# Masked attention rewritten in the form of the two unmasked layers

## The chip, the cores and the metric

The kernel runs on one core of one Trainium2 chip, in one launch. The metric is the device time of that launch in microseconds. Five engines work beside each other, each on its own queue in order: TensorE (PE; its weight loads are PEld), VectorE (DVE), ScalarE (ACT), GpSimd (POOL) and SyncE (SP), which issues most of the DMAs. Semaphores order work between the queues.

## The reference

Four blocks, each a gated cross attention followed by a gated feed-forward part, work on x of shape (16, 112, 256) with a context of shape (16, 375, 256). The change touches the second attention alone:

```python
scores = jnp.einsum('bhqd,bhkd->bhqk', q, k) * scale
scores = jnp.clip(scores, -100.0, 100.0)
scores = jnp.where(mask == 0, -jnp.inf, scores)
attn = jax.nn.softmax(scores, axis=-1)
out = jnp.einsum('bhqk,bhkd->bhqd', attn, v)
```

There are 16 heads of 16 columns. The first and third attentions are the same without clip and mask. The fourth has one head. The feed-forward parts of the first two blocks are mixtures of eight experts, of which each row uses two; the third is a feed-forward part of eight dense experts, the fourth a quantised one. All arithmetic is fp32 on the chip, apart from small bf16 helpers.

## The kernel before

One function, `attention`, makes the three many-headed layers. The context lies in SBUF for all 16 batches, transposed (`ctxT`). Layer by layer a loop runs over the batches b. Four batches form a group of queries: normalised, transposed and projected together (`norm_part`, `rows_part`, `both_queries_T`, `both_queries`). Keys and values of a batch are projected a batch or two ahead. The heads are handled in units `cp` of four: a head has 16 rows, two neighbours share 32 rows of TensorE, and the queries are masked so that one of the two counts.

The order on PE, ACT, DVE and POOL is written out by hand (`tc.manual_schedule`); only the SP queue is left to the scheduler. PSUM has two pools: three pairs of banks, `wide`, and two single ones, `bank`. A step that wants a pair waits until the third pair before it has been read out.

The unmasked layers 0 and 2 (`unmasked`) compute the scores twice. `maxima` computes them with the queries on the partitions, 112x375 a head, two heads in a pair, and VectorE reduces a pair to two negated maxima (L455). `max_parts` splits the maxima into three bf16 parts on GpSimd, and `max_rows` turns them (L475). `exponentials(b, i)`, three a batch, computes the scores again with the keys on the partitions, 125x224 a matmul into two pairs (L490), subtracts the maxima by a matmul of ones with the three parts (L502), and ScalarE takes the exponential out of PSUM (L511). `weighted` multiplies them with the values, beside which stand columns of ones, so that the sums come out too. `normalised` divides on VectorE (L545 to L553), `output` projects and adds.

The masked layer 1 (`with_mask`) computes the scores once, queries on the partitions. VectorE clips a pair and applies the mask in one pass out of PSUM (L602), then reduces it (L619). ScalarE exponentiates each head with its maximum as bias and its sum as accumulator output (L622). TensorE turns the weights, six transposes for two heads (L634), ScalarE or VectorE copies them out (L638), and `weighted_masked` multiplies with the values (L651). The inverse sums are spread to the columns on GpSimd (L666) and turned on TensorE (L675). A zero column stands behind the 375 context rows, so that a row with nothing valid stays finite.

The mixtures of layers 0 and 1 are worked off in between. `fill()` advances three generators by one step each: `route` (which expert, and scattering the rows by indirect DMA), `products` (a tile of 128 rows a step: a matmul with the expert's weights and the transpose of the next tile, one `wide` pair, L1170 and L1180) and `combine` (gather and add, L1208). A group's mixture begins when `ready` enters it, and `ensure` forces what is left of a group before the next layer needs it. So mixture work of layer 0 lies in layers 0 and 1, that of layer 1 in layers 1 and 2. The numbers of `fill()` calls decide which.

Steps that the change touches: `maxima`, `max_parts`, `max_rows`, `exponentials`, `weighted`, `output`, `mask_of`, `values_of`, `both_keys`, and the loops `unmasked` and `with_mask`.

Of the kernel before, what the change touches and what calls it, by code (L numbers as in the profile page):

```python
# [13 lines left out]
I32 = mybir.dt.int32  # L14
# [33 lines left out]
def tile_gated_xattn_stack(ctx: ExitStack, tc: tile.TileContext, a: dict, out: bass.AP):  # L48
# [22 lines left out]

    ctxZ = [ctxp.tile([P, 2, T + 1], F32, tag=f"ctx{b}", name=f"ctx{b}") for b in range(B)]
    ctxT = [t[:, :, :T] for t in ctxZ]
# [4 lines left out]
    def load_ctx(b):  # L78
        nc.gpsimd.memset(ctxZ[b][:, :, T:], 0.0)
        nc.sync.dma_start(ctxT[b], a["ctx"][:, :, b * T : (b + 1) * T])  # L80
# [173 lines left out]
    CTS = [(c, t) for c in range(2) for t in range(NT)]  # L254

    def attention(pool, layer, w):
# [6 lines left out]
        rss, uppers, valss = {}, {}, {}  # L263
        masked = layer == 1
        TK = T + 1 if masked else T
# [84 lines left out]
        def keys_of(b, c):  # L350
            if b >= B:
                return
            if c == 0:
                kTs[b] = pool.tile([P, 2, T + 1], F32, tag="kT", name=f"kT_{L}_{b}", bufs=3)
            pk = bank(f"pk_{L}_{b}_{c}")
            project(pk, w["wk"], c, ctxZ[b], TK)
            nc.scalar.activation(kTs[b][:, c, :TK], pk[:, :TK], AF.Identity, bias=w["bk"][:, c : c + 1])

        def both_keys(b):
            if b >= B:  # L360
                return
            kT = kTs[b] = pool.tile([P, 2, T + 1], F32, tag="kT", name=f"kT_{L}_{b}", bufs=3)
            pk = wide(f"pk_{L}_{b}")
            for c in range(2):
                project(pk[:, c, :], w["wk"], c, ctxZ[b], TK)
            if "bk" in w:
                for c in range(2):
                    nc.scalar.activation(kT[:, c, :TK], pk[:, c, :TK], AF.Identity, bias=w["bk"][:, c : c + 1])
            else:
                nc.scalar.copy(kT[:, :, :TK], pk[:, :, :TK])  # L370

# [26 lines left out]
        def values_of(b, ts):  # L398
# [15 lines left out]
            def copies():  # L414
                for i, t in enumerate(ts):
                    (nc.vector.tensor_copy if masked else nc.scalar.copy)(  # L416
# [12 lines left out]
        def scores(b, cp):  # L429
# [4 lines left out]
            for h in range(2):  # L434
                ps = wide(f"ps_{L}_{b}_{cp}_{h}")
                for i in range(2):
# [3 lines left out]
                        ps[:S, i, :TK],  # L440
                        qms[g][rows, c, p, j * S : (j + 1) * S],
                        kTs[b][rows, c, :TK],
# [6 lines left out]
        def maxima(b, cp):  # L449
            if b >= B:  # L450
                return
            if cp == 0:
                nms[b] = small.tile([S, 4, 4], F32, tag="nm", name=f"nm_{L}_{b}")
            for h, ps in enumerate(scores(b, cp)):
                nc.vector.tensor_reduce(nms[b][:, cp, 2 * h : 2 * h + 2], ps[:S, :, :T], AX.X, ALU.max, negate=True)  # L455

        def max_parts(b):
            if b >= B:
                return
            mp, nm = mparts[b % 2], nms[b]  # L460
            rest = nm
# [7 lines left out]
        def max_rows(b):  # L469
# [9 lines left out]
            nc.scalar.copy(mr, pt[:, : 4 * S].rearrange("p (c s) -> p c s", s=S))  # L479

        def exponentials(b, i):
# [28 lines left out]
            for h in range(2):  # L510
                nc.scalar.activation(  # L511
                    e[:, 2 * h : 2 * h + 2].rearrange("t r q p s -> t r (q p s)"), pairs[h][:TC, :, : 4 * S], AF.Exp
                )

        def weighted(b, i):
# [18 lines left out]
            if i == 2:  # L534
                by_pair = po[:, : 4 * S].rearrange("q (c p s) -> q c p s", p=2, s=S)
                valss[b] = pool.tile([P, 2, S], F32, tag="vals", name=f"vals_{L}_{b}")
# [19 lines left out]
        def output(b):  # L556
# [4 lines left out]
            if masked and b + 1 < B:  # L561

                pos[b + 1] = bank(f"po_{L}_{b + 1}")
                py = pos[b + 1][:, 2 * P :]
            else:
                py = bank(f"py_{L}_{b}")
            for c in range(2):
                nc.tensor.matmul(py[:S, :D], oT[:, c, :], w["wo"][:, c, :], start=(c == 0), stop=(c == 1))
            if not masked:
                xb = x[g][:, j, :]  # L570
                nc.vector.scalar_tensor_tensor(xb, py[:S, :D], gate[:S, layer : layer + 1], xb, ALU.mult, ALU.add)  # L571
                return
            return py

        def output_added(b, py):
            if b < 0:
                return
            g, j = divmod(b, G)
            y = pool.tile([S, D], F32, tag="y", name=f"y_{L}_{b}", bufs=1)
            nc.scalar.mul(y, py[:S, :D], gate[:S, layer : layer + 1])  # L580
# [1276 lines left out]
```

## Time and profile before

| | us |
|---|---|
| median of 7 runs (lowest to highest) | 1588.85 (1584.58 to 1593.59) |
| the profiled execution | 1585.48 |
| its span, first to last instruction | 1583.7 |
| TensorE busy | 1468.8 (93%) |
| VectorE busy | 977.6 (62%) |
| ScalarE busy | 776.2 (49%) |
| GpSimd busy | 603.4 (38%) |

The rows of groups read: line, engine, operation, output and inputs by the program's names, shapes (partitions x elements, type), count, then busy time in us, mean ns of one, and the idle time of the engine just before them with what ended it. Matmuls overlap: the busy time of a group is that of their union, and much smaller than count times mean. Every fp32 matmul of the program stands there as two records. The clock is what TensorE was granted, 1.00 is full. The timeline gives start, length, engine, line, operation and count; in brackets the idle time before and what ended it.

The stretches by layer on the profiled execution: layer 0 and the loads ahead of it end at 388.4 us, where the first scores of the masked layer begin; the scores of layer 2 begin at 868.2, the dense experts about 1222.6.

### The profile page before, as it was taken

What the parts mean: (1) busy time and instruction counts of PE and PEld (TensorE: products, weight loads), DVE (VectorE), ACT (ScalarE), POOL (GpSimd) and SP (SyncE); (2) the same over time, 40 slices, a digit from 0 to 9 for tenths busy, and PEclk for the clock granted to TensorE, in tenths of its full rate; (3) what the DMA queues carried; (4) which work ended last, traced back from release to release, by engine and by line L of the source; (5) the groups of instructions that cost most, each with busy time, mean ns of one, the idle gap of its engine ahead of it and who ended that gap; (6) DMA issues with size and microseconds to landing.
All of it is one profiled execution on the core that took longest, in us unless ns stands there. A gap on an engine that the chain in (4) does not pass through costs nothing.

```text
span 1583.7 us, 34920 instructions
## 1 busy us (share of the span) xinstructions
PE 1468.8 (93%) x13404; PEld 1023.3 (65%) x13404; DVE 977.6 (62%) x1857; ACT 776.2 (49%) x1547; POOL 603.4 (38%) x1079
## 2 busy tenths in 40 slices
PE   7999999999899899998987999999999999899997
PEld 4555666666666666766765666666566887667765
DVE  3566754666776775786683465466555434486775
ACT  2443434445666666666664344444445333465522
POOL 1222133344546545536544235342112434243342
PEclk9899999999999999999998999999999999999999
DMA  9780024253353452534513324410003441100000
GB/s 260 249 269 1 2 81 126 79 158 102 96 153 95 124 147 81 146 91 120 150 51 93 105 83 132 132 52 8 8 8 138 163 149 36 27 16 22 14 10 18
DMA packets 127214, 150.32 MB, mean 95 GB/s; under 512 B 13496, under 2 KB 118280, under 8 KB 125000
## 3 DMA queue, kind: packets, MB, share of 16 engines
q1 hardware_dynamic: 120472, 133.40, 28.5%
q0 software_dynamic: 6144, 14.69, 3.1%
q8 instruction: 106, 1.74, 0.5%
q14 instruction: 60, 0.49, 0.1%
q10 hardware_dynamic: 432, 0.01, 0.0%
HBM read 103.75 MB, written 44.30 MB: 93 GB/s over the span
## 4 chain that ended last, share of the span: by engine, by line
PE 51%; DVE 10%; POOL 5%; ACT 4%; issue 2%; DMA 1%; SPq 1%; POOLq 0%; ACTq 0%; DVEq 0%
PE ps L439 5%; PE pm_m L1170 5%; PE pv L406 4%; PE pe L634 4%; PE pk L231 4%; PE py_f L1328 3%; PE ph L1312 3%; PE pgu_h L1659 2%; PE po L651 2%; PE pt L490 2%; PE po L526 2%; DVE sm L602 2%; PE py L1693 2%; PE pq L231 1%; PE pz L1590 1%
## 5 line engine op out<-in xcount | busy, mean ns | idle before, releaser
L455 DVE TENSOR_REDUCE nm<-ps 112x2 f32<-112x750 f32 x256 | 230.1, 933 | 187.2 <-PE ps L439 186.5
L439 PE MATMUL ps<-kT,qm 32*112 32x375 f32 (+1 forms) x1536 | 213.8, 527 | 19.9 <-ACT ex L511 14.8
L511 ACT ACTIVATE ex<-pt 125x896 f32<-125x896 f32 x192 | 165.7, 914 | 70.8 <-PE pt L502 70.7
L622 ACT ACTIVATE sm<-sm,nmax 112x375 f32<-112x375 f32 x256 | 152.4, 600 | 6.6 <-DVE nmax L619 6.6
L602 DVE SCALAR_TENSOR_TENSOR sm<-ps,up 112x752 f32<-112x752 f32 x128 | 114.5, 934 | 65.6 <-PE ps L439 58.3
L634 PE MATMUL pe<-ident,sm 112*125 112x112 f32 x768 | 116.4, 286 | 29.3 <-DVE sm L602 15.1
L634 PEld LDWEIGHTS pe<-ident,sm 112*125 112x125 f32 x768 | 104.1, 196 | 57.6 <-ACT sm L622 41.9
L1170 PE MATMUL pm_m<-w_m,xy_m 128*128 128x256 f32 x416 | 117.4, 405 | 11.5 <-DVE sm L602 3.9
L439 PEld LDWEIGHTS ps<-kT,qm 32*112 32x112 f32 x1536 | 72.6, 173 | 76.7 <-ACT ex L511 33.8
L490 PE MATMUL pt<-qm,kT 32*125 32x224 f32 x1536 | 116.1, 382 | 3.7 <-DVE nm L455 2.0
L1153 POOL TENSOR_TENSOR xy_m<-xy_m,wb_m 128x256 f32<-128x256 f32 x112 | 82.2, 735 | 97.0 <-ACT xy_m L1182 96.2
L1182 ACT COPY xy_m<-pm_m 128x512 f32<-128x512 f32 x112 | 63.3, 566 | 107.2 <-PE pm_m L1180 58.4
L619 DVE TENSOR_REDUCE nmax<-sm 112x2 f32<-112x752 f32 x128 | 113.0, 923 | 0.0
L427 POOL TENSOR_SCALAR oT<-oT,w_L_xattn_bv 128x112 f32<-128x112 f32 x64 | 36.3, 575 | 191.6 <-DVE oT L553 122.4
L1170 PEld LDWEIGHTS pm_m<-w_m,xy_m 128*128 128x128 f32 x416 | 72.6, 192 | 50.4 <-ACT eT L638 15.6
L526 PE MATMUL po<-ex,vpad 125*32 125x112 f32 x3072 | 98.4, 270 | 1.6 <-ACT vpad L416 0.7
L406 PE MATMUL pv<-w_L_xattn_wv,ctx 128*125 128x256 f32 x384 | 97.4, 390 | 1.1 <-DVE x L571 1.0
L490 PEld LDWEIGHTS pt<-qm,kT 32*125 32x125 f32 x1536 | 74.7, 186 | 31.4 <-issue 12.7
L231 PE MATMUL pk<-ctx,w_L_xattn_wk 128*128 128x376 f32 (+1 forms) x256 | 93.1, 498 | 0.9 <-ACT qm L392 0.9
L638 ACT COPY eT<-pe 125x672 f32<-125x672 f32 x96 | 68.9, 718 | 51.0 <-PE pe L634 48.4
L526 PEld LDWEIGHTS po<-ex,vpad 125*32 125x32 f32 x3072 | 74.0, 113 | 28.9 <-issue 21.3
L406 PEld LDWEIGHTS pv<-w_L_xattn_wv,ctx 128*125 128x125 f32 x384 | 67.7, 188 | 23.1 <-issue 8.6
(328 smaller groups left out, 2816.5 us busy)
## 6 DMA issues: line engine op xcount, KB each, us to landing
w_m<-in_L_ffn_expert_w_dram SPq DMA_DIRECT2D x112, 256.0 KB, 3.8
w<-in_L_ffn_w_dram SPq DMA_DIRECT2D x16, 1024.0 KB, 5.8
xg_m<-rows_in SPq DMA_DIRECT2D x112, 128.0 KB, 2.7
wb_m<-in_L_ffn_expert_b_dram SPq DMA_DIRECT2D x112, 128.0 KB, 3.8
rows_out<-xy_m SPq DMA_DIRECT2D x112, 128.0 KB, 1.8
rows_in<-zero SPq DMA_DIRECT2D x2, 4992.0 KB
rows_out<-zero SPq DMA_DIRECT2D x2, 4992.0 KB
ctx<-in_ctx_dram SPq DMA_DIRECT2D x16, 375.0 KB, 9.5
```

The lines of the kernel that those rows point to most:

```text
L231: nc.tensor.matmul(ps[:, :n], w[:, k, c * P : (c + 1) * P], rhs[:, k, :n], start=(k == 0), stop=(k == 1))
L406: nc.tensor.matmul(pv[:TC, i * D : (i + 1) * D], rhs_of(b)[:, k, t * TC : (t + 1) * TC], w["wv"][:, k, :], start=(k == 0), stop=(k == 1),)
L439: nc.tensor.matmul(ps[:S, i, :TK], qms[g][rows, c, p, j * S : (j + 1) * S], kTs[b][rows, c, :TK], start=True, stop=True,)
L455: nc.vector.tensor_reduce(nms[b][:, cp, 2 * h : 2 * h + 2], ps[:S, :, :T], AX.X, ALU.max, negate=True)
L490: nc.tensor.matmul(pairs[r // 2][:TC, r % 2, q * 2 * S : (q + 1) * 2 * S], kTs[b][rows, c, t * TC : (t + 1) * TC], qms[g][rows, c, :, j * ...
L511: nc.scalar.activation(e[:, 2 * h : 2 * h + 2].rearrange("t r q p s -> t r (q p s)"), pairs[h][:TC, :, : 4 * S], AF.Exp)
L526: nc.tensor.matmul(po[32 * r : 32 * r + 32, (2 * c + p) * S : (2 * c + p + 1) * S], vp[:, t, 4 * c + r, p : p + 2, :], e[:, r, q, p, :], s ...
L602: nc.vector.scalar_tensor_tensor(sm[:, 2 * h : 2 * h + 2, :], ps[:S, :, :TK], -100.0, uppers[b][:, None, :].to_broadcast([S, 2, TK]), ALU.max,
L619: nc.vector.tensor_reduce(part, sm[:, 2 * h : 2 * h + 2, :], AX.X, ALU.max, negate=True)
L622: nc.scalar.activation(sm[:, i, :T], sm[:, i, :T], AF.Exp, bias=nmax[:, i : i + 1], accum_out=rss[b][:, head : head + 1])
L634: nc.tensor.transpose(pt[:TC, i, t * S : (t + 1) * S], sm[:, 2 * h + i, t * TC : (t + 1) * TC], ident[:S, :S])
L1170: nc.tensor.matmul(pt[:, 1, :D], xgT[:, k * P : (k + 1) * P], w[:, k * D : (k + 1) * D], start=(k == 0), stop=(k == 1),)
```

## The change

The masked layer takes the form of the two others; one loop, `run`, serves all three. What differs in it for the masked layer:

- The mask of a batch is loaded one batch ahead (`load_mask`), and GpSimd turns it into a bf16 tile `ups` of 0 and -1e30 (one pass in place of two and a memset).
- `maxima`: one fused instruction a head adds that tile to the scores and takes the maximum, 16 a batch in place of eight reductions. The sum goes to a scratch tile `over` of one buffer. In the changed program's order each stands as two instructions, the pass and a read of the accumulator into `nm`, and most passes wait for an earlier instruction of VectorE's own queue.
- `max_parts` first clips the maxima to between -20 and 100 on GpSimd.
- `max_rows` also turns the mask (four bf16 transposes, one third twice, so that any two neighbouring thirds stand side by side) and ScalarE copies it twice.
- `exponentials`: VectorE clips and masks what the two matmuls left in PSUM in one pass (at least -80, at most 0 or -1e30) and writes it to SBUF; ScalarE takes the exponential there in place.
- The value copies of the masked layer go to ScalarE. The zero column of the context is gone.

In the shared loop, layers 1 and 2 start the norm of the next group one batch later (`when`), batch 15 has two more `fill()`s in every layer, and the masked layer one more in every fourth batch. A masked batch has five `fill()`s, each fourth six; before it had six.

```diff
+    LOW = 20.0
...
             for h, ps in enumerate(scores(b, cp)):
-                nc.vector.tensor_reduce(nms[b][:, cp, 2 * h : 2 * h + 2], ps[:S, :, :T], AX.X, ALU.max, negate=True)
+                if not masked:
+                    nc.vector.tensor_reduce(nms[b][:, cp, 2 * h : 2 * h + 2], ps[:S, :, :T], AX.X, ALU.max, negate=True)
+                    continue
+                for i in range(2):
+                    r = 2 * h + i
+                    over = pool.tile([S, T], F32, tag="over", name=f"over_{L}_{b}_{cp}_{r}", bufs=1)
+                    nc.vector.tensor_tensor_reduce(
+                        over, ps[:S, i, :T], ups[b], 1.0, -3.0e38, ALU.add, ALU.max, nms[b][:, cp, r : r + 1]
+                    )
...
+            if masked:
+
+                rest = small.tile([S, 4, 4], F32, tag="left", name=f"cut_{L}_{b}")
+                nc.gpsimd.tensor_scalar(rest, nms[b], -LOW, 100.0, ALU.max, ALU.min)
...
+            up = ups.pop(b)
+            for i in range(4):
+                t = i % NT
+                nc.tensor.transpose(pt[:TC, (4 + i) * S : (5 + i) * S], up[:, t * TC : (t + 1) * TC], identb[:S, :S])
+            nc.scalar.mul(mr, by_unit, -1.0)
+            uT = uTs[b] = pool.tile([TC, 4, 2, S], BF16, tag="uT", name=f"uT_{L}_{b}")
+            for p in range(2):
+                nc.scalar.copy(uT[:, :, p, :], pt[:TC, 4 * S : 8 * S].rearrange("t (i s) -> t i s", s=S))
...
             for h in range(2):
-                nc.scalar.activation(
-                    e[:, 2 * h : 2 * h + 2].rearrange("t r q p s -> t r (q p s)"), pairs[h][:TC, :, : 4 * S], AF.Exp
-                )
+                eh = e[:, 2 * h : 2 * h + 2]
+                less = pairs[h][:TC, :, : 4 * S]
+                if masked:
...
+                    t = CTS[2 * i][1]
+                    eh = eh.rearrange("t r q p s -> t r (q p s)")
+                    u = uTs[b][:, t : t + 2].rearrange("t q p s -> t (q p s)")
+                    nc.vector.scalar_tensor_tensor(
+                        eh, less, LOW - 100.0, u[:, None, :].to_broadcast([TC, 2, 4 * S]), ALU.max, ALU.min
+                    )
+                    nc.scalar.activation(eh, eh, AF.Exp)
+                    continue
+                nc.scalar.activation(eh.rearrange("t r q p s -> t r (q p s)"), less, AF.Exp)
...
+        def load_mask(b):
+            if masked and b < B:
+                mks[b] = pool.tile([S, T], I32, tag="mk", name=f"mk_{L}_{b}", bufs=1)
+                nc.sync.dma_start(mks[b], a["mask_Bx1xSxS2_ik1"][b, 0])
 
         def mask_of(b):
...
+            if masked and b < B:
+                ups[b] = pool.tile([S, T], BF16, tag="upper", name=f"up_{L}_{b}")
+                nc.gpsimd.tensor_scalar(ups[b], mks.pop(b), 0, -BIG, ALU.is_equal, ALU.mult)
+                load_mask(b + 1)
...
-        def masked_scores(b, cp):
...
-        def with_mask(nxt):
...
-        def unmasked(nxt, block):
+        def run(nxt):
 
             first = layer == 0
+            when = 1 if first else 2
...
             for b in range(B):
                 g, at = b // G + 1, b % G
+                mask_of(b + 2)
                 exponentials(b, 0)
...
-                if at == 1:
-                    if b > 1:
-                        ready(layer, g - 2)
+                if at == 1 and b > 1:
+                    ready(layer, g - 2)
+                if at == when:
                     ensure(layer - 1, g)
...
                 exponentials(b, 1)
                 weighted(b, 0)
+                if masked and at == 3:
+                    fill()
                 maxima(b + 1, 3)
```

In the loop of `run` one batch reads, with the names of the steps: first exponential block, output of batch b-2, third maximum of batch b+1, fill, values, normalisation of batch b-1, second block, weighted, fourth maximum, keys, fill, weighted, first maximum of batch b+2, fill, turned maxima, third block, second maximum, values, fill, weighted, fill.

## The prediction

> **What bounds the kernel now.** I read the page first, then busy time by stretches, then TensorE's groups and waits inside the masked layer, then one batch of an unmasked layer in order of time. The stretches are cut where the scores of layer 0, 1 (the masked one) and 2 begin; the last begins at the dense part.
>
> ```profile
> span 1583.7 us, 34920 instructions
> PE 1468.8 (93%) x13404; PEld 1023.3 (65%) x13404; DVE 977.6 (62%) x1857; ACT 776.2 (49%) x1547; POOL 603.4 (38%) x1079
> ```
>
> ```profile
> 388.40:868.20 479.80, 433.59 (x3836) 312.01 (x3836) 337.64 (x639) 299.79 (x770) 245.62 (x366) 0.96 0.40 112
> 868.20:1222.60 354.40, 336.58 (x3904) 219.47 (x3905) 201.14 (x351) 161.64 (x260) 110.27 (x222) 0.99 0.25 73
> ```
>
> The columns of the second fence are length, then busy time of PE, PEld, DVE, ACT, POOL, then clock, DMA share, GB/s. The masked layer takes 479.8 us, the third 354.4. TensorE is the busiest engine in both, with 46 us idle in the masked layer and 18 in the third. Which work differs, and what TensorE waits for:
>
> ```profile
> L634 PE MATMUL pe<-ident,sm 112*125 112x112 f32 x768 | 116.4, 286 | 29.3 <-DVE sm L602 15.1 <-ACT sm L622 14.1
> L602 DVE SCALAR_TENSOR_TENSOR sm<-ps,up 112x752 f32<-112x752 f32 x128 | 114.5, 934 | 65.6 <-PE ps L439 58.3 <-POOL up L594 3.9 <-POOL apart_m L1084 3.3
> L619 DVE TENSOR_REDUCE nmax<-sm 112x2 f32<-112x752 f32 x128 | 113.0, 923 | 0.0
> L490 PE MATMUL pt<-qm,kT 32*125 32x224 f32 x768 | 57.1, 376 | 1.6 <-DVE nm L455 0.7
> L502 PE MATMUL pt<-mr,onesb 3*125 3x224 bf16 x384 | 22.2, 254 | 0.0
> L455 DVE TENSOR_REDUCE nm<-ps 112x2 f32<-112x750 f32 x128 | 115.0, 933 | 93.4 <-PE ps L439 93.4
> L1570 DVE SCALAR_TENSOR_TENSOR sm<-ps,mask 112x375 f32<-112x375 f32 x16 | 8.7, 543 | 17.6 <-PE ps L1566 17.5
> ```
>
> The first three rows are the masked layer's, the next three the third's, the last the final block's. The 768 transposes cost TensorE 116.4 us; computing scores a second time costs 57.1 + 22.2 = 79.3. That saving is what speaks for the change.
>
> In the unmasked form one batch runs so (start, length; TensorE, then VectorE):
>
> ```profile
> 912.91 0.37 PE L502 MATMUL pt<-mr,onesb 3*125 3x224 bf16 x8
> 913.10 0.80 PE L439 MATMUL ps<-kT,qm 32*112 32x375 f32 x4
> 914.28 0.89 PE L439 MATMUL ps<-kT,qm 32*112 32x375 f32 x4 [0.38 <-ACT ex L511]
> ...
> 918.96 0.37 PE L502 MATMUL pt<-mr,onesb 3*125 3x224 bf16 x8
> 919.26 0.97 PE L526 MATMUL po<-ex,vpad 125*32 125x112 f32 x32
> 920.16 1.05 PE L439 MATMUL ps<-kT,qm 32*112 32x375 f32 x8
> 921.14 2.79 PE L231 MATMUL pk<-ctx,w_L_xattn_wk 128*128 128x375 f32 x8
> ...
> 918.81 0.44 DVE L545 TENSOR_SCALAR sums<-po,hsel 128x224 f32<-128x224 f32 x1
> 919.29 0.45 DVE L546 SCALAR_TENSOR_TENSOR sums<-po,hsel,sums 128x224 f32<-128x224 f32 x1
> 919.66 0.44 DVE L548 SCALAR_TENSOR_TENSOR vals<-po,hsel,vals 128x224 f32<-128x224 f32 x1
> ...
> 922.04 0.39 DVE L553 TENSOR_TENSOR oT<-vals,inv 128x224 f32<-128x224 f32 x1
> 922.35 1.78 DVE L455 TENSOR_REDUCE nm<-ps 112x2 f32<-112x750 f32 x2
> ```
>
> Three things to see. The second score pair of a maximum waits until ScalarE has exponentiated the first pair of the block before it: there are only three PSUM pairs. From the end of the first exponential block (913.10) to the keys (921.14) TensorE needs 8.04 us. And VectorE's normalisation takes 3.54 us (918.81 to 922.35); here nothing on TensorE waits for it, since the exponentials leave PSUM through ScalarE.
>
> **The template.** The masked layer takes the third's form, so I start from the third's 354.4 us. A mixture tile holds TensorE about 1.2 us (915.09 to 916.28 in that timeline, 923.76 to 924.94). Of the 112 mixture products 27 fall in the third's stretch (108 matmul records, four a product) and one routing, about 3.3 us of TensorE. Without them: 354.4 - 32.4 - 3.3 = 318.7. By the changed instruction order 56 products and four routings fall into the new masked layer: 318.7 + 67.2 + 13.2 = 399.1. The six products fewer than now (62) are run beside other layers, 6 x 1.2 = 7.2 us there. Were the added VectorE work hidden, the kernel would change by 399.1 + 7.2 - 479.8 = -73.5 us.
>
> **What is added to the template.**
>
> 1. Four transposes of the bf16 mask a batch, at the 0.074 us at which the four of the maxima follow one another: 0.3 x 16 = 4.8 us, on TensorE's path.
>
> 2. The fused maximum: 16 a batch in place of eight reductions, and each is two instructions, a pass and a read of the accumulator. The pass I take from the 112x375 row, 0.543, which has the same shape and sources (bounds: 0.47, half the reduction of 750 elements, and 0.93, half the rate). The read is not in the trace on VectorE: ScalarE's takes 0.191, VectorE's smallest operations 0.135 (the 8x1 copies). The scratch tile has one buffer, so each pass waits for the one before: an instruction with such a wait starts 0.034 after its predecessor's end, one without 0.083 before (the second and third VectorE lines above). A head then takes 0.46 + 0.135 + 0.034 = 0.63; bounds are 0.58, if the read hides behind the wait, and 0.69 with ScalarE's read. A pair takes 1.26, a reduction now 0.85 start to start.
>
> [...]
>
> 3. Clip and mask: six passes a batch of 125x896 from PSUM. From 0.543 at 375 and 0.934 at 752 elements the slope is 1.037 ns, so 1.08 each, 1.00 start to start (bounds: 0.93, the 752-element row, and 1.30, the 375-element row scaled). Queued behind a pass are ScalarE's exponential, and TensorE's next score pair, which needs that PSUM pair. VectorE's queue is in order, so the second block's clips wait for the normalisation. From the end of the first block: 0.2 to start, clips 2.0, output addition 0.4, four heads 2.52, normalisation 3.54, clips 2.08, release 0.06: 10.8 us until TensorE may write the keys, against 8.04.
>
> VectorE's mixture and norm work goes ahead of that normalisation too. In the changed order, over four batches, these stand there: a routing's statistics 2.1 and two additions 0.8; the norm's statistics 2.1; the placing 1.5; together 6.5, or 1.6 a batch. The middle so costs 10.8 + 1.6 - 8.04 = 4.4 us a batch more.
>
> Later in the batch the last block's clip holds the next score pair 0.17 longer than ScalarE's 0.914 did, and two maxima ahead of the block end about 0.25 late: 0.4. Together 4.8 x 14 batches = 67. Batch 14 pays a middle, 4.0, batch 15, which has no maxima left, its clips behind the normalisation, 2.5: 6.5. The opening has eight pairs before the first block, 0.41 longer each: 3.
>
> 4. TensorE's clock. After gaps of 2.54 and 2.81 us the trace grants half the clock for 3.4 us (0.51 from 445.5 to 449.0); after one of 5.12 for 10.3. A hole of 2.4 to 5 us stands in every batch of the new form, before the fourth pair and the keys. I take one half-clock stretch in two batches: 7 x 1.7 = 12. The bounds are none and every batch, 24. [...]
>
> At nothing: the eight reductions a batch of the clipped scores, VectorE's weight and value copies, ScalarE's 256 exponentials with accumulator reads (the template holds what replaces them); two ScalarE copies of the turned mask, about 0.53 each, beside ScalarE's 10 us a batch (161.64 / 16) in a batch of 30; GpSimd's clip of the maxima, about 0.25, in the 4 us between the last maximum and its transpose, which a burst of indirect DMAs (0.97 each) can use up. The mask's load moves one batch ahead; on SP it waits for GpSimd's conversion (1.52), and mixture loads queue behind it, covered by being issued two tiles early; a late conversion of 3 us would still be covered. The zero column costs TensorE one of 376 columns.
>
> **Sum.** 399.1 + 4.8 + 67 + 6.5 + 3 + 12 = 492.4, and 7.2 elsewhere: 499.6 against 479.8, +20. The profiled execution took 1585.48 (span 1583.7), 3.4 below the median; on the median, 1588.85 + 20 = 1609.
>
> **Rivals.** (a) Faster: the holes are filled. TensorE runs up to three pairs ahead, and where a mixture tile falls in the hole it costs nothing; if statistics and additions mostly arrive outside it (-22) and the clock holds (-12), 1609 - 34 = 1575. It decides at 3.4 us a batch instead of 4.8. For it: TensorE's work falls by some 40 us. Against: three pairs are all there are. With no stall at all the time would be near 1521.
>
> (b) VectorE is the bound outright. A batch has 16 x 0.63 + 6.0 + 3.54 + 0.4 + routing, adding and norms 4.1 = 24.2 us, on a period of 30. Were a fused pass 0.2 longer than 0.543, 3.2 x 14 = 45 more: 1654. [...]
>
> (c) The fused maximum doesn't do what it says, since it is two instructions and a wait where one reduction stood; this is in the forecast already, and alone is 0.41 x 8 x 14 = 46 us of VectorE work, half of it hidden.
>
> **How the numbers follow.** Forecast with its bounds (1594 to 1630): 0.52. Rival (a) 0.26, 0.05 of it within 0.3% of before; (b) 0.14; the forecast's terms at the low ends of their bounds, close to no change, 0.08, 0.06 of it within 0.3%. About 0.3%, 4.8 us, is what a measurement of this kernel can tell from no change. So faster 0.21, same 0.11, slower 0.68. Leaving out the far ends of (a) and (b), the range is 1565 to 1642; the forecast's own is 1594 to 1630.
>
> **What would show it.** Right: score pairs and keys wait for the clip passes, by 2 us or more a batch; the transposes are gone; VectorE is above 75% busy in the masked layer, at a period near 30 us; half-clock stretches there are more frequent. Wrong: TensorE's waits in that layer stay near the third's 18 us; the accumulator read costs nothing, or a pass is far from 0.54.

## The result, and the profile after

The changed kernel takes 1660.7 us in the median (1643.9 to 1667.4), the kernel before beside it 1590.0: 1.044 times, 95% interval 1.042 to 1.046. It is slower, as forecast, but by 71 us instead of 20, and outside the range given. Chips differ: the kernel before took 1588 to 1591 us on three of those used and 1618 and 1623 on two others, so each ratio is against the kernel before on the same chip, and lengths of layers are compared within the first three unless another chip is named.

The page of the changed kernel (its own time 1667.6) opens so; then come its layers, cut where the scores of layer 1 and 2 begin and where the dense part does, and the third layer of the kernel before, cut in the same way (length, busy time of PE, PEld, DVE, ACT, POOL, clock, DMA share, GB/s):

```profile
span 1665.9 us, 35780 instructions
PE 1515.3 (91%) x13884; PEld 1021.7 (61%) x13884; DVE 1005.5 (60%) x2225; ACT 684.1 (41%) x1115; POOL 587.9 (35%) x1091
```

```profile
398.70:920.70 522.00, 448.61 (x4271) 292.19 (x4270) 356.95 (x987) 203.88 (x330) 207.76 (x364) 0.90 0.32 92
920.70:1298.80 378.10, 354.59 (x3903) 228.22 (x3902) 204.06 (x358) 159.33 (x255) 128.48 (x248) 0.94 0.26 74
```

```profile
868.20:1216.30 348.10, 331.03 (x3878) 214.70 (x3878) 197.62 (x344) 157.60 (x252) 108.45 (x219) 0.99 0.24 69
```

The masked layer takes 522 us where 480 stood and 492 were forecast. TensorE idles 73 us in it (46 before), and the clock that it is granted is 0.90 (0.96 before): summed over the clock's records, 109 us at half speed instead of 34. The third layer has grown too. (In the kernel before, the dense part's first products start at 1216.3 us, not at 1222.6: the 354.4 us of the prediction's template hold 6.3 us of the dense part.)

What VectorE costs and what TensorE waits for, in the masked layer:

```profile
L449 DVE CUSTOM_DVE_ANT_0 over<-ps,up 112x375 f32<-112x375 f32 x256 | 139.9, 546 | 89.9 <-PE ps L427 75.6 <-DVE nm L449 0.7
L530 DVE SCALAR_TENSOR_TENSOR ex<-pt,uT 125x896 f32<-125x896 f32 x96 | 100.1, 1084 | 48.7 <-PE pt L512 48.7
L449 DVE DVE_READ_ACCUMULATOR2_ANT nm<- 112x1 f32 x256 | 21.2, 83 | 0.0
```

```profile
PE ps L427 <- DVE ex L530: 36.0, 23, 4.3
PE pm_m L1018 <- DVE nm L449: 7.8, 6, 1.8
```

The prices were right: a fused pass 0.546 us (0.543 forecast), a clip pass 1.084 (1.08). The accumulator read takes 0.083, less than the 0.135 assumed, and a head 0.59 start to start instead of 0.63. The wait is the one forecast, of score pairs (L427) for clip passes (L530): 36 us in 23 waits, or 2.6 for each of 14 batches. One such hole, and what follows it, on TensorE and then on VectorE:

```profile
585.53 0.89 PE L427 MATMUL ps<-kT,qm 32*112 32x375 f32 x4
590.76 1.59 PE L427 MATMUL ps<-kT,qm 32*112 32x375 f32 x4 [4.34 <-DVE ex L530]
592.28 5.07 PE L228 MATMUL pk<-ctx,w_L_xattn_wk 128*128 128x375 f32 x8
```

```profile
584.67 0.39 DVE L813 BATCH_NORM_STATS2 st_m<-x 112x6 f32<-112x256 f32 x1
...
585.19 0.97 DVE L1056 SCALAR_TENSOR_TENSOR x<-yg_m,picks_m,x 112x256 f32<-112x256 f32 x2
586.09 0.45 DVE L567 TENSOR_SCALAR sums<-po,hsel 128x224 f32<-128x224 f32 x1
...
587.29 1.54 DVE L571 RECIPROCAL sums<-sums 128x224 f32<-128x224 f32 x1
...
589.62 2.08 DVE L530 SCALAR_TENSOR_TENSOR ex<-pt,uT 125x896 f32<-125x896 f32 x2
```

The second score pair waits 4.34 us, because the clip that frees its PSUM stands behind statistics, two additions and the normalisation. Then come the keys, which cost more than the hole seems to: at a granted clock of 0.53 (590.1 to 597.4) they take 5.07 us where the kernel before shows 2.79.

### The profile page after: what moved, and what is told of

The parts are those of the page before. It is cut to its first block, busy times and chain, and to the rows that moved or that the text cites. A ratio compares the mean times of both kernels' runs of the same rounds, so it can differ in the third digit from the quotient of the medians.

```text
span 1665.9 us, 35780 instructions
## 1 busy us (share of the span) xinstructions
PE 1515.3 (91%) x13884; PEld 1021.7 (61%) x13884; DVE 1005.5 (60%) x2225; ACT 684.1 (41%) x1115; POOL 587.9 (35%) x1091
## 5 line engine op out<-in xcount | busy, mean ns | idle before, releaser
L427 PE MATMUL ps<-kT,qm 32*112 32x375 f32 x1536 | 252.1, 543 | 60.7 <-DVE ex L530 36.0
L500 PE MATMUL pt<-qm,kT 32*125 32x224 f32 x2304 | 187.3, 401 | 11.8 <-DVE nm L449 4.2
L449 DVE CUSTOM_DVE_ANT_0 over<-ps,up 112x375 f32<-112x375 f32 x256 | 139.9, 546 | 89.9 <-PE ps L427 75.6
L427 PEld LDWEIGHTS ps<-kT,qm 32*112 32x112 f32 x1536 | 86.0, 178 | 142.4 <-DVE ex L530 53.6
L500 PEld LDWEIGHTS pt<-qm,kT 32*125 32x125 f32 x2304 | 120.2, 196 | 58.8 <-issue 21.0
L548 PE MATMUL po<-ex,vpad 125*32 125x112 f32 x4608 | 150.2, 273 | 5.3 <-ACT ex L533 2.1
L533 ACT ACTIVATE ex<-ex 125x896 f32<-125x896 f32 x96 | 91.1, 950 | 126.1 <-DVE ex L530 124.2
L530 DVE SCALAR_TENSOR_TENSOR ex<-pt,uT 125x896 f32<-125x896 f32 x96 | 100.1, 1084 | 48.7 <-PE pt L512 48.7
L228 PE MATMUL pk<-ctx,w_L_xattn_wk 128*128 128x375 f32 x256 | 105.2, 561 | 3.8 <-ACT qm L380 1.9
L404 ACT COPY vpad<-pv 125x256 f32<-125x256 f32 x144 | 49.0, 375 | 137.2 <-PE pv L394 136.7
L228 PEld LDWEIGHTS pk<-ctx,w_L_xattn_wk 128*128 128x128 f32 x256 | 53.7, 220 | 54.7 <-issue 13.7
```

The costliest lines, as they stand in the source:

```text
L228: nc.tensor.matmul(ps[:, :n], w[:, k, c * P : (c + 1) * P], rhs[:, k, :n], start=(k == 0), stop=(k == 1))
L427: nc.tensor.matmul(ps[:S, i, :T], qms[g][rows, c, p, j * S : (j + 1) * S], kTs[b][rows, c, :T], start=True, stop=True,)
L449: nc.vector.tensor_tensor_reduce(over, ps[:S, i, :T], ups[b], 1.0, -3.0e38, ALU.add, ALU.max, nms[b][:, cp, r : r + 1])
L500: nc.tensor.matmul(pairs[r // 2][:TC, r % 2, q * 2 * S : (q + 1) * 2 * S], kTs[b][rows, c, t * TC : (t + 1) * TC], qms[g][rows, c, :, j * ...
L530: nc.vector.scalar_tensor_tensor(eh, less, LOW - 100.0, u[:, None, :].to_broadcast([TC, 2, 4 * S]), ALU.max, ALU.min)
L533: nc.scalar.activation(eh, eh, AF.Exp)
```

## The experiments

A number from one profile is that run's. All six traces from the two slower chips show waits whose releaser the profile calls remote, 22 to 59 us in sum over the engines; none of the fourteen other traces has one. What releases these waits stays open. The first two runs below, the first without the clip and the first with the plain maximum come from one of those chips; the last two of these were repeated on another.

### Is it the later norm?

The batches in which the next group's norm now stands are the longest of the masked and third layers (37 to 39 us in the masked one), and the forecast had not priced its new place (`when`). Three runs move it. In the changed kernel, all layers early:

```
-            when = 1 if first else 2
+            when = 1
```

> The changed kernel with the layer norm of the next four batches done at the second batch of each four, as in the kernel before, in all three layers (when = 1). Theory 'late norm' (the forecast gave no price to the norm's later place; the batches in which it now stands, every fourth, are the longest ones of both the masked and the third layer, 38 to 40 and 28 to 35 us): the third layer's stretch falls from 378 by 16 to 25, the masked layer's from 522 by 10 to 20, and the whole from 1661 to 1616 to 1635. Theory 'holes and clock' (the passes that hold PSUM make the holes, and the half clock after them, 104 us at half in the masked layer against 34 before, is what was under-priced): the holes are all still there, so 1653 to 1669.

Measured: 1.053 times the kernel before (1.049 to 1.056), on a slower chip, on which the changed kernel itself was not run. Two versions below were run there and on another chip, and their ratios are 0.016 higher there (1.005 and 0.989, 1.040 and 1.024). By that, an estimate of the changed kernel there is 1.060, and some 11 us may have come back. They are in the third layer, 379.6 us against 391.0 and 391.7 in those two versions. The masked layer has 550.3; the changed kernel's 522 and the 22 to 28 us that the same two took longer there make 544 to 550, so nothing came back in it.

The kernel before, with the late place (when = 2, and the queries moved accordingly) in its third layer alone:

```
+            when = 1 if first else 2
...
-                if at == 1:
+                if at == when:
                     ensure(layer - 1, g)
...
-                if at == 2:
+                if at == when + 1:
                     bias_part(g, range(G))
```

> The kernel before, with only the norm's later place (when = 2) put into its third layer. Theory 'late norm': the third layer's stretch grows from 348 to 365 to 375, the whole by 16 to 25. Theory 'holes and clock': there are no VectorE passes on PSUM pairs behind it, so the whole moves by 0 to 6.

Measured: 1.010 (1.006 to 1.015), on the same chip: some 16 us slower, at the lower end of what 'late norm' expected, and near the 11 of the run above. The third is from a chip without the remote waits:

```
-            when = 1 if first else 2
+            when = 2 if masked else 1
```

> The changed kernel with the norm's place as it was (one batch earlier) in the third layer alone. If the late norm is what the forecast missed in that layer (its stretch: 348 in the kernel before, 369 to 378 in the changed one, 363 where only its norm was early beside other edits), the stretch comes back to 358 to 366 and the whole by 8 to 12, 1.036 times the kernel before. If the layer grew by its two more mixture tiles and by the clock alone, nothing moves: 1.042 to 1.046.

Measured: 1.043 (1.038 to 1.048), the changed kernel's own ratio. The third layer:

```profile
920.10:1286.30 366.20, 346.03 (x3903) 224.25 (x3902) 202.20 (x358) 159.08 (x255) 127.61 (x248) 0.95 0.26 77
```

366 us against 369 and 378 in two profiles of the changed kernel. The clock varies by more than that there, so half of the half-clock time is taken off: what is left is 354 to 356 us in the eight profiles with the late norm, from chips without the remote waits, and 349 to 351 in the five with the early one. The later norm costs some 5 us in that layer, waits for the queries' copies among it (5.8 us against 0.9), and isn't where the 50 us went. In the masked layer only the first of the three runs moves it.

### The two VectorE additions, apart and together

First the changed kernel again, for a comparison on one chip:

> The changed kernel itself, run beside the following three and beside the kernel before on the same chip, so that differences of a few us can be read. 1.042 to 1.046 times the kernel before.

Measured: 1.044 (1.037 to 1.050). Its profile has span 1651.2; in the masked layer, 522.1 us, TensorE is idle for 73.3, and the clock is at half for 109.2. The third layer:

```profile
915.00:1284.10 369.10, 345.14 (x3904) 222.42 (x3903) 204.03 (x358) 159.24 (x255) 128.24 (x248) 0.96 0.26 76
```

Without the clip and mask pass:

```
-                    nc.vector.scalar_tensor_tensor(
-                        eh, less, LOW - 100.0, u[:, None, :].to_broadcast([TC, 2, 4 * S]), ALU.max, ALU.min
-                    )
-                    nc.scalar.activation(eh, eh, AF.Exp)
+                    nc.scalar.activation(eh, less, AF.Exp)
```

> The changed kernel without the clip and mask pass: ScalarE exponentiates straight from PSUM, so the weights are neither clipped nor masked. This takes VectorE off the release of the PSUM pairs of the exponentials. Theory 'holes and clock': masked layer from 522 to 435 to 450 (45 us of idle and 40 of half clock go), half-clock time there under 45 us, the whole 1570 to 1590. Theory 'late norm': only the forecast's price of the clips goes, 4 us a batch, the whole near 1605, and half-clock stretches stay in every fourth batch. Theory 'VectorE is the bound': the layer falls by the busy time of the passes, 96 x 1.08 = 104, to 418.

> The changed kernel without the clip and mask pass (weights neither clipped nor masked) once more, beside the two others. If the prices add, as in the forecast: with 105 us for both and 6 to 8 for the maximum, it is 97 to 99 faster than the changed kernel, 0.98 times the kernel before. If the fused maximum's price shows only when the clips no longer hold the PSUM pairs: 60 to 75 faster, 0.996 to 1.005.

Without the fused maximum:

```
-                for i in range(2):
...
-                    nc.vector.tensor_tensor_reduce(
-                        over, ps[:S, i, :T], ups[b], 1.0, -3.0e38, ALU.add, ALU.max, nms[b][:, cp, r : r + 1]
-                    )
+                nc.vector.tensor_reduce(nms[b][:, cp, 2 * h : 2 * h + 2], ps[:S, :, :T], AX.X, ALU.max)
```

> The changed kernel with one plain reduction of 750 elements in place of two fused passes with their two reads, so the mask is left out of the maximum (it stays in the weights). VectorE's work falls by 8 x (1.28 - 0.85) = 3.4 us a batch, 55 us in all. Theory 'holes and clock': half of it lies on the path and takes as much clock with it, 25 to 40 faster, 1620 to 1636. Theory 'late norm': 15 to 25, 1636 to 1646. Theory 'VectorE is the bound': 50 or more, under 1611.

> The changed kernel with one plain reduction of 750 in place of two fused passes (mask left out of the maximum) once more. If the prices add and the clips are worth 60 to 65: 40 faster than the changed kernel, 1.018. If it is hidden behind the clips: 3 to 10 faster, 1.037 to 1.042.

And without both:

> The changed kernel with both VectorE additions gone: ScalarE exponentiates straight from PSUM (weights neither clipped nor masked) and one plain reduction of 750 takes the place of two fused passes (the mask left out of the maximum). What is left is the third layer's form plus the mask's transposes. The forecast's template: 399.1 + 4.8 for the masked layer and 7.2 elsewhere against 479.8, 0.957 times the kernel before. If instead the two effects measured one by one simply add (62 and 6 to 7 off the changed kernel), 1.000 to 1.004: then the template was short by about 70, and the forecast's terms for VectorE had to be too large to come out at +20.

Measured on the slower chip: 1.005 without the clip, 1.040 with the plain maximum. On the others: 0.989 (0.985 to 0.992) without the clip, 1.024 (1.020 to 1.027) with the plain maximum, 0.978 (0.975 to 0.981) with neither. Their masked layers, in that order:

```profile
391.50:825.60 434.10, 398.38 (x4274) 267.43 (x4273) 260.03 (x891) 195.16 (x330) 207.93 (x364) 0.96 0.40 110
```

```profile
395.40:887.80 492.40, 432.97 (x4271) 284.86 (x4270) 331.18 (x603) 203.83 (x330) 207.83 (x364) 0.92 0.34 97
```

```profile
392.20:809.90 417.70, 390.12 (x4273) 263.05 (x4272) 235.02 (x507) 195.22 (x330) 207.61 (x364) 0.98 0.40 114
```

From 522.1 the clips alone bring 88 us, the maximum alone 30, both 104: some 13 us count twice. In none of these three runs did an expected ratio come out; the expectations of the repeated runs rested on the slower chip's differences. But the first clip run's theory 'holes and clock' named 435 to 450 us for the masked layer, with under 45 at half clock, and the repeated run has 434.1 and 30.7; 'VectorE is the bound' named 418.

With neither addition, idle time falls to 27.6 us and half clock to 13.7. So of the 104 us, 45.7 are idle time, at most (109.2 - 13.7) / 2 = 47.8 are time lost to the half clock (TensorE is busy in 100 of the 109 us), and 11 or a little more I can't assign. And the template, the third layer's form without VectorE's additions, is measured: 417.7 against 403.9 (399.1 and 4.8 for the transposes).

### Is the clock lost to the holes?

Idle products are put on TensorE where its largest holes stand:

```
+                if masked:
+                    for k in range(32):
+                        nc.tensor.matmul(
+                            pos[b][:, 4 * S :], identb, identb[:, : 512 - 4 * S], start=True, stop=True, skip_group_check=True
+                        )
                 maxima(b + 1, 3)
```

> The changed kernel with 32 idle bf16 products of 64 columns a batch, into PSUM columns that nothing reads, placed on TensorE ahead of the fourth pair of a maximum, where its holes of 2 to 4.3 us stand; some 2 us a batch, 30 us in all, if they ran beside nothing. If the holes themselves cost the clock: half-clock time in the masked layer falls from 109 us to under 65, and the time by that gain of 22 or more less the filler that stands where no hole was: 10 faster to 5 slower than the changed kernel, although work was added. If the clock falls for another reason, half-clock time stays at 95 to 120 us and the kernel is 15 to 34 slower.

Measured: 1.041 (1.036 to 1.046); idle time 62 us, half clock 106, the layer 521.8 us. The products took 1.2 us a batch, not 2, and a hole of 3.3 us was left of 4.3. That tells nothing of the clock. (They start a new accumulation in the bank of the weighted sums, and with them this kernel's output isn't the attention's, with a relative error of 0.17; the next ones only accumulate.) With 96 in place of 32:

```
-                    for k in range(32):
+                    for k in range(96):
...
-    start=True, stop=True
+    start=False, stop=False
```

> The changed kernel with 96 idle bf16 products a batch where there were 32 (0.03 us each in that run at full clock, so 2.9 us a batch, 40 in all), accumulated into PSUM columns that nothing reads. The holes of 4.3 us shrink to 1.4, those of 2 are closed. If the holes cost the clock: half-clock time in the masked layer falls from 106 to 109 us to under 70, and although up to 20 us of the filler stand where no hole was, the layer is no longer than 522. If the half clock has another cause: half-clock time stays above 95 us and the layer grows by 10 to 25 us.

Measured: 1.041 (1.037 to 1.044). The place shown above now reads:

```profile
586.73 2.97 PE L702 MATMUL po<-identb 128*128 128x64 bf16 x96
...
591.95 0.89 PE L427 MATMUL ps<-kT,qm 32*112 32x375 f32 x4 [1.44 <-DVE ex L530]
592.95 2.79 PE L228 MATMUL pk<-ctx,w_L_xattn_wk 128*128 128x375 f32 x8
```

The keys are back at 2.79 us. In the layer 42 us of work were added; idle time fell by 21 us, half-clock time from 109 to 78.5, and the length stayed at 521.7. So these holes do cost the clock, and filling them pays for most of the filler: 21 us of idle time and at most (109.2 - 78.5) / 2 = 15 of clock; the 6 that are left I can't assign. Under 70 us at half clock was expected, and above 95 if the half clock had another cause.

### Other orders, and a version that might win

The clips of the second block ahead of the normalisation:

```
-                normalised(b - 1)
+                if not masked:
+                    normalised(b - 1)
                 exponentials(b, 1)
+                if masked:
+                    normalised(b - 1)
```

> The changed kernel with the masked layer's normalisation of the batch before put behind the second block's clips in VectorE's order; no work is added or removed. Theory 'holes and clock': the hole before the keys and the fourth pair shrinks by up to the 3.5 us of the normalisation in each batch, a part of it comes back in the wait for the maxima behind it; half-clock time in the masked layer falls from 109 us to under 75, the whole by 25 to 45 against the changed kernel. Theory 'VectorE is the bound' (its sum of work sets the pace): within 6 us of the changed kernel.

Measured: 1.037 (1.030 to 1.043), masked layer 511, 95.6 us of it at half clock: some 11 us faster than the changed kernel, between the two expectations. The wait for the clip fell from 36 to 11 us, and another came, of mixture tiles for the maxima that now stand behind the normalisation (7.8 before):

```profile
PE pm_m L1021 <- DVE nm L449: 20.0, 13, 1.8
```

Then versions in which ScalarE exponentiates straight from PSUM and VectorE multiplies the mask in afterwards, in SBUF, so that the weighted sum waits for it instead of PSUM. `uT` then holds 1 and 0, since ScalarE takes its exponential when it copies the turned mask out:

```
-                nc.scalar.copy(uT[:, :, p, :], pt[:TC, 4 * S : 8 * S].rearrange("t (i s) -> t i s", s=S))
+                nc.scalar.activation(uT[:, :, p, :], pt[:TC, 4 * S : 8 * S].rearrange("t (i s) -> t i s", s=S), AF.Exp)
...
-                    nc.vector.scalar_tensor_tensor(
-                        eh, less, LOW - 100.0, u[:, None, :].to_broadcast([TC, 2, 4 * S]), ALU.max, ALU.min
-                    )
-                    nc.scalar.activation(eh, eh, AF.Exp)
+                    nc.scalar.activation(eh, less, AF.Exp)
...
+                    nc.vector.tensor_tensor(eh, eh, u[:, None, :].to_broadcast([TC, 2, 4 * S]), ALU.mult)
```

> ScalarE exponentiates straight from PSUM; VectorE then multiplies the exponentials in SBUF by the mask as 0 or 1, with as many passes of the same size as the clip had, issued just before the weighted sum that reads them, and the normalisation of the batch before goes behind the first of them. The lower and upper clip of the scores are left out. The norm's place is late (when = 2) in the masked layer alone and early in the third. Theory 'holes and clock': VectorE does as much as before but no longer holds a PSUM pair of the exponentials; masked layer 455 to 475 and 12 to 16 back in the third: 0.99 to 1.005 times the kernel before. Theory 'VectorE is the bound': the masked layer stays at 515 or more, and only the third layer's 12 to 16 come back: 1.033 to 1.037.

Measured: 1.056 (1.052 to 1.060), the worst of these versions, and slower than either expected ratio. The products stand in VectorE's queue behind the maxima, and TensorE's weighted sums wait for them at once:

```profile
PE po L551 <- DVE ex L546: 63.8, 68, 4.0
```

With the weighted sums one step later (`times` holds the two products; this cut and the next show the masked layer's order and leave the conditions out), and then with the plain maximum of above as well:

```
                 exponentials(b, 0)
+                weighted(b - 1, 2)
...
                 maxima(b + 1, 2)
+                times(b, 0)
...
                 exponentials(b, 1)
+                normalised(b - 1)
-                weighted(b, 0)
                 maxima(b + 1, 3)
                 max_parts(b + 1)
+                times(b, 1)
                 both_keys(b + 2)
+                weighted(b, 0)
...
                 exponentials(b, 2)
+                weighted(b, 1)
                 maxima(b + 2, 1)
+                times(b, 2)
```

> As the run that multiplied the mask in after the exponential, with each weighted sum one step later in TensorE's order, so that the two multiplying passes have a step's time, and the normalisation behind the second block's scores. The fused masked maximum stays; the clip of the scores is left out. Theory 'a VectorE pass costs where TensorE waits for it, not by its sum': masked layer 440 to 470, the third 358 to 366, 0.985 to 1.005 times the kernel before. Theory 'VectorE is the bound': the masked layer stays above 500, 1.03 and more.

> The same with one plain reduction of 750 in place of two fused passes and their reads, so the mask is left out of the maximum as well as the clip out of the scores; the mask still zeroes the weights. VectorE has 30 us less to do in the layer. First theory: masked layer 425 to 445, 0.975 to 0.985 times the kernel before. Second: 470 to 490, 1.00 to 1.01.

Measured: 1.034 (1.029 to 1.040), masked layer 511; and 1.018 (1.010 to 1.025), masked layer 481. The next wait in the second is for GpSimd's parts of the maxima:

```profile
PE pm L469 <- POOL mparts L457: 16.1, 5, 4.5
```

In both, the masked layer came out where 'VectorE is the bound' had put it (above 500, 470 to 490). And the layer does follow VectorE's work: without the clip, with the plain maximum and with neither, VectorE is busy 97, 26 and 122 us less, and the layer is 88, 30 and 104 shorter. But the order counts as well, at nearly the same work: VectorE is busy 357, 357, 362 and 369 us in the changed kernel, with the clips first, and in the two versions with the products and the fused maximum, and the layer takes 522, 511, 545 and 511. It idles for 142 us or more in each. So its sum of work is not the bound; what counts is where TensorE waits for it.

The normalisation behind those maxima; then, on top of it, half of the products on GpSimd; then, instead of that, one pass for two:

```
-                normalised(b - 1)
                 maxima(b + 1, 3)
                 max_parts(b + 1)
+                normalised(b - 1)
                 times(b, 1)
```

> The version with the mask multiplied in after the exponential, delayed weighted sums and the plain maximum (clip left out of the scores, mask out of the maximum), with the normalisation moved behind the fourth pair's maxima, so that GpSimd's parts and TensorE's transposes of them no longer wait for its 3.5 us. If that wait (16 us of TensorE's idle time, and the clock after it) is the last of weight: masked layer from 481 to 445 to 460, 0.995 to 1.005 times the kernel before. If another wait takes its place (the output's, for the normalised values): 470 to 480, 1.010 to 1.017.

```
-                nc.vector.tensor_tensor(eh, eh, u[:, None, :].to_broadcast([TC, 2, 4 * S]), ALU.mult)
+                eng = nc.gpsimd if h else nc.vector
+                eng.tensor_tensor(eh, eh, u[:, None, :].to_broadcast([TC, 2, 4 * S]), ALU.mult)
```

> The version with the normalisation behind the fourth pair's maxima (mask multiplied in after the exponential, delayed weighted sums, plain maximum; clip left out of the scores, mask out of the maximum), with the second of each two multiplying passes on GpSimd. From the 128x256 product there (0.73 us) an estimate of 2.6 us a pass, 7.7 us a batch on GpSimd, and 3.2 us a batch less on VectorE. If VectorE's work makes what is left: masked layer from 481 to 440 to 455, 0.985 to 1.0 times the kernel before. If GpSimd's passes stand ahead of the parts of the maxima, which TensorE's transposes wait for: 475 to 500, 1.01 to 1.03.

```
-            for h in range(2):
...
+            nc.vector.tensor_tensor(eh, eh, u[:, None, :].to_broadcast([TC, 4, 4 * S]), ALU.mult)
```

> The same version with one multiplying pass of 125x1792 on VectorE in place of two of 125x896. 48 instructions fewer in the layer, each with a wait of 0.03 to 0.1 us: 3 to 5 us of VectorE. If the number of instructions counts: masked layer 472 to 478, 1.008 to 1.012. If the latency counts, since the one pass waits for both exponentials and the first weighted sums wait for the whole of it: 481 to 490, 1.015 to 1.02.

Measured: 1.015 (1.011 to 1.018); with GpSimd's share 1.015 (1.012 to 1.018) and with one pass for two 1.019 (1.015 to 1.023), these two on a slower chip, on which the first was not run; what they gain over it stays open. In the first the wait for the parts fell from 16.1 to 8.6 us, and TensorE's idle time only from 64 to 61. No version that applies the mask to the weights reached the kernel before; the 0.978 above is what a mask without VectorE's work would give.

## Why the prediction was right in direction and wrong in size

Against the profile of span 1651.2, 67.5 us above the kernel before's 1583.7, the sum closes so:

| | forecast | measured | short by |
|---|---|---|---|
| template and transposes, masked layer | 403.9 | 417.7 | 13.8 |
| VectorE's additions, stalls | 76.5 | 45.7 idle, 11 unassigned | |
| VectorE's additions, half clock | 12 | 47.8 at most | |
| the two together | 88.5 | 104.4 | 15.9 |
| outside the masked layer | 7.2 | 25.2 | 18.0 |
| change of the kernel | +20 | +67.5 | 47.7 |

- **Clip, fused maximum, own-queue wait: right.** Each price within 0.06 us (a pass started 0.035 us after the end of the read before it, 0.034 forecast). The place and the kind of wait are the forecast's, the transposes are gone and half-clock stretches are more frequent. One sign failed: VectorE is busy 68% of the masked layer (357 of 522 us) at a period of 32.6 us, not above 75% at 30.
- **Step 4, TensorE's clock: the term that failed.** It took one stretch of 3.4 us at half clock in two batches, seven in all. The trace has twenty in 16 batches, 5.5 us long on average: 109 us at half speed. With the 13.7 us taken off that are there without VectorE's additions, they cost up to 47.8 us where 12 were forecast. The step's upper bound, 24, was too low as well: it let each stretch last 3.4 us, although the trace before showed 10.3 us after one hole.
- **The stall terms were too large** (76.5 against 46 to 57), which hides part of the miss of the clock. The step that added stalls and clock as if they were apart may be behind both, since at half clock TensorE's own work takes longer (the keys above 5.07 us instead of 2.79) and may have covered waiting; no run shows that. The two additions were also treated as separate costs; they overlap by some 13 us.
- **The template was 14 us short**, and 20 without the 6.3 us of the dense part that it held. With neither addition TensorE idles 27.6 us; the third layer's 354 us had 18. I took the third layer's idle time unchanged into a layer with twice its mixture work. In that run TensorE's longest waits are still for PSUM, 10.2 us of score pairs for ScalarE, and 6.1 of mixture tiles for the maxima.
- **"7.2 elsewhere" was 25.** The third layer grew by 21: three more products (18 more matmul records, six a product, 3.6 us at 1.2), 7 idle, and up to (27.3 - 9.6) / 2 = 9 of clock; the later norm's 5 us are in these. The stretch up to the masked layer grew by 4.5. The clock there is no firm amount: the eight profiles with the late norm have 20 to 48 us at half in it.
- **The later norm was not costed at all.** It is worth some 5 us in the third layer; in the masked one no run shows that it weighs.
- **The rivals.** (a) TensorE's work did fall (433.6 to 390.1 us with neither addition), but the holes were not filled. (b) gave 1654, near the result, by luck: its condition, a fused pass 0.2 us longer than 0.543, did not come, and VectorE idles for 165 us of the masked layer. (c) was in the forecast; the maximum alone is worth 30 us, where half of 46 was forecast.
- **The range** ended at 1642. Three terms failed together, all upward: the clock by up to 36 us, the time outside the masked layer by 18 and the template by 14. The stalls, 20 to 31 too large, made up for only part of it.

## What to carry to other kernels

In this program a wait on TensorE of 2 us or more costs itself and then, as a rule, the clock (of 98 such waits at full clock in fourteen profiles, away from the program's ends, 91 were followed by half clock within 3.5 us; in the profiles of the kernel before and the changed kernel, 14 of 15): count the holes of a batch, and price each with the work that follows it at half speed. A template taken from a quieter stage has to be given the idle time of the busier one. And before a costly operation is moved off PSUM, ask what stands ahead of it on the engine that gets it, as statistics, additions and the normalisation stood ahead of the clip in the hole of 4.34 us: here multiplying the mask in later made the kernel slower, until the consumer was moved as well.

## What the runs showed of the hardware

- **The granted clock changed on a grid of 3.41 us.** In the profiles of the kernel before and the changed kernel all half-clock stretches, 16 and 34, start on one such grid each, and last one to five times 3.41 us (the one at 590.1 us in the changed kernel 6.83), but for the last of each profile, which the end cuts. Over the fourteen profiles from chips without the remote waits, the stretches of full clock were cut into windows of that length, and the idle time of TensorE in each was summed. Of 4476 windows with less than 0.4 us, 5 were followed by half clock; of 1147 with 0.4 to 1.2, 125; of 249 with 1.2 to 1.8, 126; of 122 with more, 119, among them all 85 with 2 us or more. In the profiles of the kernel before and the changed kernel alone the four counts are 642 and 0, 173 and 14, 29 and 20, 18 and 16. So in these profiles little more than half a window's idle time (1.8 us) was nearly always followed by half clock.
- **The spread of the runs goes with the clock.** The eight runs of the changed kernel with a mean clock of 0.938 took 1665.7 to 1667.6 us, the two with 0.951 took 1643.9 and 1648.2.
- **Beside VectorE's products of two SBUF tiles GpSimd's instructions took longer.** These are its bias addition of 128x112 and its addition of 128x256, in the masked layer of the changed kernel and then of the version with the normalisation last:

```profile
L1001 POOL TENSOR_TENSOR xy_m<-xy_m,wb_m 128x256 f32<-128x256 f32 x56 | 40.7, 730 | 95.0 <-ACT xy_m L1030 94.5
...
L415 POOL TENSOR_SCALAR oT<-oT,w_L_xattn_bv 128x112 f32<-128x112 f32 x32 | 17.9, 569 | 70.9 <-DVE oT L575 66.2 <-DVE lg_m L850 4.7
```

```profile
L1023 POOL TENSOR_TENSOR xy_m<-xy_m,wb_m 128x256 f32<-128x256 f32 x56 | 50.5, 907 | 72.6 <-ACT xy_m L1052 72.1
...
L415 POOL TENSOR_SCALAR oT<-oT,w_L_xattn_bv 128x112 f32<-128x112 f32 x32 | 35.6, 1118 | 29.2 <-DVE oT L576 24.7 <-DVE lg_m L872 3.0 <-DMA w_m<-in_L_ffn_expert_w_dram 1.5
```

  0.73 became 0.91 and 0.57 became 1.12 us. In that layer the ten profiles without the products, the kernel before among them, have means of 0.73 to 0.74 and 0.57 to 0.58 us, the six with them 0.82 to 0.91 and 0.62 to 1.12. With half of the products on GpSimd, one took 1.96 us there (2.6 was estimated), and VectorE's own rose from 1.08 to 1.31. What makes them longer, no run shows.
